# Second graph-attention layer: the logits of a block's first three columns made by TensorE, a block ahead

## Chip, cores and metric

One Trainium2 chip, one of its cores. The metric is the device time of one execution in microseconds, the median of several runs. Engines are named as in the profile: PE (TensorE, with PEld its weight loads), DVE (VectorE), ACT (ScalarE), POOL (GpSimd), SP (the queue that issues plain DMAs).

## The reference

A graph of 6250 nodes with 256 features each and 100000 directed edges, sorted by destination. Two layers of attention of one kind (GATv2, four heads of 64), a residual and a layer norm, then one layer of another kind (eight heads of 32), a residual and a layer norm:

```
def _gatv2_layer(x, src, dst, n, Wl, Wr, att, b):
    xl = (x @ Wl).reshape(n, 4, 64);  xr = (x @ Wr).reshape(n, 4, 64)
    e = leaky_relu(xl[src] + xr[dst], 0.2)
    logits = einsum('ehc,hc->eh', e, att)
    ex = exp(logits - segment_max(logits, dst)[dst])
    alpha = ex / segment_sum(ex, dst)[dst]
    return segment_sum(xl[src] * alpha[:, :, None], dst).reshape(n, 256) + b

h = elu(_gatv2_layer(x, ..., Wl1, Wr1, att1, b1))      # layer 1, with an edge from each node to itself
h = _gatv2_layer(h, ..., Wl2, Wr2, att2, b2)           # layer 2, the same edges
x = layernorm(x + h)
x = layernorm(x + third_layer(x, W, a, src, dst))      # a GAT layer with logits s1[src] + s2[dst]
```

The change concerns the line `logits = ...` of layer 2.

## The kernel before

All arithmetic is in float32. A plan made at the start sorts the nodes by the number of their edges, most first, and cuts them into 49 blocks of 128. A block's nodes lie on the 128 partitions, and a block has as many columns as its nodes may have edges, and one more ahead of them (column 0) for the node's own row: 28 in block 0, then 26, 25, 24, 23, 22, 22, 21 (three blocks), 20 (four), 19 (four), 18 (four), 17 (five), 16 (five), 15 (five), 14 (four), 13 (three), 12 (two), 11 (two) and 10 in block 48. The few edges of block 0 that do not fit are dealt with apart (the `few_...` names).

A column's rows are fetched by one indirect DMA of POOL (`gather_rows`, L1300): 128 rows of 260 numbers, four heads of 64 and a 65th each, which carries the linear part of the leaky ReLU. Column 0 isn't gathered; ACT copies it from a tile `two` (L1712), which SP loads. The columns of a block are cut into two to four tiles `g` of at most nine columns, as equal as can be, from one pool of nine such tiles. So the gathers run ahead of the arithmetic until all nine are full.

`layer2` is called twice, with i=0 for layer 1 and i=1 for layer 2. The order of instructions on every engine is the order in which the program is written; each engine works off its own queue and waits only for the data that it needs. One turn of the loop over blocks b does, in this order:

1. the gathers of block b+1 are issued, and `own2` copies its destination rows `xr` into PSUM (`ready`, L1711);
2. `attend(b)`: for each tile, DVE takes the maximum of the rows and `xr` (L1573), multiplies by the attention vector `at` (L1574) and sums each head (L1575) into the logits `lg`; then DVE takes the largest (`top`, L1439), and ACT the exponentials, one call a head (L1446), into `wt`. After them ACT copies some of the weights (`by`, L1453) and, from the list `later`, the own row of block b+1 into column 0 of that block's first tile (L1712);
3. `end(b - 1)`: DVE divides the last block's sum `acc` by `den` (L1602), adds the residual (L1715) and takes its mean and variance (L1516, L1518), and ACT the reciprocal of the deviation (L1520, L1521);
4. DVE's reciprocal of `den` (L1638), and `weighted_sum`: DVE multiplies the first tile by its weights (L1477); then comes the call `between()`, in which DVE makes the shift of the layer norm (`sd`, L1525) and ACT applies it (L1528); then the other tiles, of the last one a part by ACT (L1476). PE sums the columns into `acc` with an identity (L1484);
5. PE turns the normalised block (L1420) and multiplies it for the third layer (L1427), ACT copies the result out (L1726) and SP stores it (L1728).

PSUM tiles for turning and for products come from one pool `pst`, with the tag `tp`, of two buffers that are used in turn.

The third layer gathers rows that the second one stored. For its first three blocks 37 gathers (`begin`, from the call `follow`) need no rows of the last four blocks; the others wait for all of them.

Of the kernel before, what the change touches and what calls it, by code (L numbers as in the profile page):

```python
# [26 lines left out]
F32 = mybir.dt.float32  # L27
# [3 lines left out]
OP = mybir.AluOpType  # L31
AX = mybir.AxisListType
# [3 lines left out]
P = 128  # L36
# [4 lines left out]
RUNS = 64  # L41
EARLY = (14, 12, 11)
LATE = 4


def columns(E, N, NB):
# [1161 lines left out]
def tile_by_degree(  # L1208
# [3 lines left out]
    nc = tc.nc  # L1212
    N, F = x.shape
    H2, D2 = att1.shape
    H1, _, D1 = w3.shape
    NB = -(-N // P)
    NP = NB * P
    T = 9
    A1 = F + H1
    W2 = H2 * (D2 + 1)  # L1220
    CM = near_d.shape[1] - F
# [8 lines left out]
    def per_head(t, H):  # L1230
        return t.rearrange("p (h d) -> p h d", h=H)
# [9 lines left out]

    AHEAD = (NB - LATE) * P
    KEY = max(cols).bit_length()
# [4 lines left out]
                   allow_small_or_imprecise_dtypes=True)  # L1248
# [3 lines left out]
                   allow_small_or_imprecise_dtypes=True)  # L1252
# [42 lines left out]
    def gather_rows(b, rows, cut, own, table, of, width, j0, j1):  # L1295


        for g, (s0, s1) in zip(rows, cut):
            for j in range(max(s0 - own, j0), min(s1 - own, j1)):
                nc.gpsimd.indirect_dma_start(  # L1300
                    out=g[:, j + own - s0, :width], out_offset=None, in_=table,
                    in_offset=source(of, b, j),
                )
# [31 lines left out]
    def gather_few(table, j, width):  # L1335
        nc.gpsimd.indirect_dma_start(
            out=few_row[:, :width], out_offset=None, in_=table,
            in_offset=bass.IndirectOffsetOnAxis(ap=few_at[:, j : j + 1], axis=0),
        )
# [38 lines left out]
    def row_tiles(b, own):  # L1378
        cut = chunks(cols[b] + own)
        return [rowp.tile([P, T, RW], F32, name="g") for _ in cut], cut  # L1380
# [149 lines left out]
    def layer2(i, table, of, width, start, own, finish, follow):  # L1530

        with ExitStack() as es:
            zp = es.enter_context(tc.tile_pool(name=f"z{i}", bufs=1))
            work = es.enter_context(tc.tile_pool(name=f"work{i}", bufs=3))
            ps = es.enter_context(tc.tile_pool(name=f"ps{i}", bufs=2, space=PSUM))
            ps1 = es.enter_context(tc.tile_pool(name=f"ps1{i}", bufs=1, space=PSUM))  # L1540
            pst = es.enter_context(tc.tile_pool(name=f"pst{i}", bufs=2, space=PSUM))
            at = ps1.tile([P, W2], F32, name="at")
            nc.scalar.copy(at, att[i])
            state = {}

            def gather(b):
                first = EARLY[b] if b in begun else 0
                rows, cut = begun.pop(b) if first else row_tiles(b, 1)
                gather_rows(b, rows, cut, 1, table, of, width, first, cols[b])
                if b == 0:  # L1550
                    gather_few(table, i, width)
                state[b] = [rows, cut]

            later = []

            def ready(b):
                pr, put = own(work, ps, pst, b, state[b][0][0][:, 0, :W2])
                state[b].append(pr)
                later.append(put)

            def attend(b):
                rows, cut, xr = state.pop(b)
                S = cols[b] + 1
                lg = work.tile([P, CM + 1, H2], F32, name="lg")
                if b == 0:
                    own_r = work.tile([P, W2], F32, name="few_own", bufs=1)
                    nc.scalar.copy(own_r, xr)
                    po = pst.tile([P, W2], F32, name="few_r", tag="tp")
                    nc.tensor.matmul(po, node_of, own_r, start=True, stop=True)
                for g, (s0, s1) in zip(rows, cut):  # L1570
                    n = s1 - s0
                    z = zp.tile([P, T, W2], F32, name="z")[:, :n, :]
                    nc.vector.tensor_max(z, g[:, :n, :W2], xr[:, None, :].to_broadcast([P, n, W2]))  # L1573
                    nc.vector.tensor_mul(z, z, at[:, None, :].to_broadcast([P, n, W2]))  # L1574
                    nc.vector.reduce_sum(  # L1575
                        lg[:, s0:s1, :], z.rearrange("p t (h d) -> p t h d", h=H2), axis=AX.X
                    )
                if b == 0:
                    none(po)
                    z = zp.tile([P, T, W2], F32, name="z")[:, 0, :]  # L1580
                    nc.vector.tensor_max(z, few_row[:, :W2], po)
                    nc.vector.tensor_mul(z, z, at)
                    few_lg = work.tile([P, H2], F32, name="few_lg", bufs=1)
                    nc.vector.reduce_sum(few_lg, per_head(z, H2), axis=AX.X)
                    few_logits(work, pst, lg, few_lg, H2)
                    if i == 0:
                        nc.vector.tensor_copy(few_at[:, 1:], few_row[:, W2 : W2 + 1])
                few = min(S // 3, cut[-1][1] - cut[-1][0] - 1) if b + 1 < NB else 0
                wt, new = weights(work, ps, lg, S if b else S + FEW, H2, few, S)
                while later:  # L1590
                    later.pop()()
                if i == 0:
                    for g, (s0, s1) in zip(rows, cut):
                        s = max(s0, 1)
                        nc.scalar.copy(spots[:, b, s - 1 : s1 - 1], g[:, s - s0 : s1 - s0, W2])
                    if 0 < b <= len(EARLY):
                        sort_sources(work, pst, b - 1)
                return rows, cut, wt, new

            def end(b, acc, den):  # L1600
                h = work.tile([P, F], F32, name="h")
                nc.vector.tensor_mul(  # L1602
                    per_head(h, H2), per_head(acc, H2),
                    den.unsqueeze(2).to_broadcast([P, H2, D2]),
                )
                if i == 0:
                    nc.vector.tensor_add(h, h, bias[0])
                return finish(work, pst, b, h)

            for b in range(3):  # L1610
                if (i, b) not in loaded:
                    start(b)
            if i == 0:
                find_few(work, pst)
            gather(0)
            ready(0)
            later.pop()()
            if i == 0:
                none(state[0][2])
            acc, den, rest = None, None, None  # L1620
            for b in range(NB):
                if b + 3 < NB:
                    start(b + 3)
                if b + 1 < NB:
                    gather(b + 1)
                if b + 2 == NB:
                    follow()
                if b + 1 < NB:
                    ready(b + 1)
                rows, cut, wt, new = attend(b)  # L1630
                if b:
                    rest = end(b - 1, acc, den)
                else:
                    few = few_sum(work, pst, wt[0], cols[0] + 1, H2, D2 + 1)
                if i == 0:
                    nc.vector.tensor_add(x1[:, b, :], x1[:, b, :], bias[1])
                den = new()
                nc.vector.reciprocal(den, den)  # L1638

                last = []  # L1640

                def between():
                    if b:
                        last.append(rest())

                acc = weighted_sum(
                    ps1, rows, cut, wt, H2, D2 + 1, between, b == 0,
                )
                if b == 0:
                    nc.tensor.matmul(acc, edges_of, few, start=False, stop=True)  # L1650
                if i == 0 and b + 1 < NB:
                    none(state[b + 1][2])
                if last:
                    last[0]()
            end(NB - 1, acc, den)()()

    def none(t):

        nc.vector.memset(t.rearrange("p (h d) -> p h d", h=H2)[:, :, D2:], -BIG)
# [76 lines left out]
    def begin2():  # L1736
        begin(1, xl2_d, W2)
        for b in range(3):
            start2(b)
            loaded.add((1, b))  # L1740

    layer2(0, xl1_d[:, :], sources, W2 + 1, start1, own1, finish1, begin2)
    last_weights()
    layer2(1, xl2_d[:, :], spots, W2, start2, own2, finish2, lambda: begin(0, wh_d, A1))

    with ExitStack() as es:
        work = es.enter_context(tc.tile_pool(name="work3", bufs=3))
        ps = es.enter_context(tc.tile_pool(name="ps3", bufs=3, space=PSUM))
        state = {}
# [59 lines left out]
        for b in range(NB):  # L1809
# [4 lines left out]
            rows, cut, wt, new = attend(b)  # L1814
# [46 lines left out]
```

## Time and profile before

| | |
|---|---|
| median of 3 runs | 3349.63 us (3349.41 to 3349.76) |
| the profiled execution | 3349.41 us, span 3347.6 us |
| busy, share of the span | DVE 85%, POOL 73%, PE 40%, PEld 32%, ACT 31% |
| layer 2 on DVE | from 1241.85 us (first maximum, block 0) to 2294.82 us (last statistics) |
| first third-layer gather that needs the last rows | 2302.9 us |
| gathers, L1300 | 0.95 us each |
| L1573, L1574, L1575, both layers | 497 us busy each, 234 instructions each |

A profile shows one execution. A group's row gives line, engine, operation, what is written and read, and the count, then busy time and the mean of one, then the idle time of the engine ahead of it and what ended that. A row of the timeline gives start, duration, engine, line and shape. In a row of waits stand the engine and line that waited, what it waited for, the total in us, how often, and the longest. "issue" is time in which an engine waited for nothing that the profile shows. PEclk is the share of full clock that PE was granted.

### The profile page before, as it was taken

What the parts mean: (1) busy time and instruction counts of PE and PEld (TensorE: products, weight loads), DVE (VectorE), ACT (ScalarE), POOL (GpSimd) and SP (SyncE); (2) the same over time, 40 slices, a digit from 0 to 9 for tenths busy, and PEclk for the clock granted to TensorE, in tenths of its full rate; (3) what the DMA queues carried; (4) which work ended last, traced back from release to release, by engine and by line L of the source; (5) the groups of instructions that cost most, each with busy time, mean ns of one, the idle gap of its engine ahead of it and who ended that gap; (6) DMA issues with size and microseconds to landing.
All of it is one profiled execution on the core that took longest, in us unless ns stands there. A gap on an engine that the chain in (4) does not pass through costs nothing.

```text
span 3347.6 us, 23565 instructions
## 1 busy us (share of the span) xinstructions
PE 1350.1 (40%) x5129; PEld 1076.3 (32%) x5130; DVE 2858.4 (85%) x2674; ACT 1048.7 (31%) x4176; POOL 2439.5 (73%) x2588
## 2 busy tenths in 40 slices
PE   7355665666667753554545555553000000000000
PEld 6244554555555543443434444442000000000000
DVE  7699999999999979999999999995976666666766
ACT  3133444444454532443444444451000000000000
POOL 5477777777777777777777777647777777777775
PEclk8678888888888876777777777776555555555555
DMA  8744444444444454444444444434433343333333
GB/s 203 145 111 117 117 121 118 119 120 121 122 122 122 123 137 111 121 121 123 114 126 127 126 126 127 112 94 114 108 107 108 107 108 108 107 108 107 108 107 86
DMA packets 189101, 395.81 MB, mean 118 GB/s; under 512 B 56249, under 2 KB 107963, under 8 KB 188934
## 3 DMA queue, kind: packets, MB, share of 16 engines
q0 software_dynamic: 121392, 339.19, 38.8%
q1 hardware_dynamic: 59858, 53.27, 5.5%
q10 hardware_dynamic: 7700, 1.74, 0.4%
q8 instruction: 45, 0.74, 0.1%
q14 instruction: 106, 0.87, 0.1%
HBM read 354.02 MB, written 40.42 MB: 118 GB/s over the span
## 4 chain that ended last, share of the span: by engine, by line
POOL 21%; DVE 20%; issue 14%; DMA 3%; PE 2%; ACT 2%; DVEq 0%; POOLq 0%; ACTq 0%
POOL g L1300 20%; DVE z L1574 5%; DVE z L1573 5%; DVE lg L1575 5%; PE acc L1484 2%; DVE g L1477 2%; DMA g<-xl_d,near_r 2%; ACT wt L1446 2%; POOL out L1800 1%; DMA out<-y,node_i 1%; DVE weighted L1497 1%; DMA g<-whs_d,near_r 0%; DVE top L1439 0%; DVE acc_v L1506 0%; DVE sd L1525 0%
## 5 line engine op out<-in xcount | busy, mean ns | idle before, releaser
L1300 POOL DMA_INDIRECT g<-xl_d,near_r x1569 | 1487.7, 948 | 518.6 <-issue 425.8
L1484 PE MATMUL acc<-g,ident 128*128 128x256 f32 x3408 | 968.0, 454 | 750.1 <-DVE sd L1525 443.1
L1484 PEld LDWEIGHTS acc<-g,ident 128*128 128x128 f32 x3408 | 787.7, 234 | 931.1 <-issue 478.3
L1300 POOL DMA_INDIRECT g<-whs_d,near_r x766 | 726.8, 949 | 233.9 <-issue 226.9
L1573 DVE TENSOR_TENSOR z<-g,pr 128x1820 f32<-128x1820 f32 (+4 forms) x234 | 497.2, 2125 | 20.8 <-DMA g<-xl_d,near_r 7.4
L1574 DVE TENSOR_TENSOR z<-z,at 128x1820 f32<-128x1820 f32 (+4 forms) x234 | 497.5, 2126 | 8.0
L1575 DVE TENSOR_REDUCE lg<-z 128x28 f32<-128x1820 f32 (+4 forms) x234 | 497.3, 2125 | 8.1
L1476 ACT ACTIVATE g<-g,by 128x64 f32<-128x64 f32 x2056 | 500.0, 334 | 0.0
L1477 DVE TENSOR_TENSOR g<-g,wt 128x1792 f32<-128x1792 f32 (+8 forms) x234 | 348.3, 1505 | 2.7
L1506 DVE TENSOR_REDUCE acc_v<-weighted 128x256 f32<-128x4096 f32 (+15 forms) x49 | 343.7, 7014 | 1.6
L1446 ACT ACTIVATE wt<-lg,top 128x19 f32<-128x19 f32 (+14 forms) x392 | 115.3, 294 | 496.3 <-DVE top L1439 460.2
L1456 ACT ACTIVATE wt<-lg 128x128 f32<-128x128 f32 (+17 forms) x49 | 14.0, 285 | 802.0 <-DVE lg L1455 802.0
L1770 DVE TENSOR_TENSOR lg<-g,s_r 128x56 f32<-128x56 f32 (+4 forms) x111 | 22.4, 214 | 268.1 <-DMA g<-whs_d,near_r 212.3
L1497 DVE TENSOR_TENSOR weighted<-g,wt 128x1792 f32<-128x1792 f32 (+4 forms) x111 | 226.6, 2057 | 0.1
L1422 ACT COPY xT<-pt 128x256 f32<-128x256 f32 x147 | 55.0, 374 | 498.0 <-PE pt L1420 498.0
L1427 PE MATMUL pm<-wcat,xT 128*128 128x260 f32 x392 | 100.8, 401 | 22.6 <-ACT xT L1422 22.6
L1427 PEld LDWEIGHTS pm<-wcat,xT 128*128 128x128 f32 x392 | 71.5, 192 | 43.4 <-ACT xT L1422 34.4
L1446 ACT ACTIVATION_READ_ACCUMULATOR wt<-lg,top 128x1 f32 x392 | 73.1, 186 | 0.0
L1800 POOL DMA_INDIRECT out<-y,node_i x49 | 50.0, 1021 | 25.9 <-issue 14.2
L1427 PE MATMUL pm<-wh_cat,xT 128*128 128x272 f32 x196 | 58.8, 423 | 22.6 <-ACT xT L1422 22.6
L1427 PE MATMUL pl<-wcat,xT 128*128 128x260 f32 x196 | 57.4, 416 | 25.2 <-ACT xT L1422 25.2
L1691 ACT COPY row<-pm 128x260 f32<-128x260 f32 x98 | 36.6, 374 | 86.9 <-PE pm L1427 86.9
(247 smaller groups left out, 1436.8 us busy)
## 6 DMA issues: line engine op xcount, KB each, us to landing
g<-xl_d,near_r POOLq DMA_INDIRECT x1569, 2.8
g<-whs_d,near_r POOLq DMA_INDIRECT x766, 2.8
whs_d<-row SPq DMA_DIRECT2D x49, 132.0 KB, 2.0
xl_d<-xl SPq DMA_DIRECT2D x49, 130.0 KB, 6.0
xl_d<-row SPq DMA_DIRECT2D x49, 130.0 KB, 2.5
xr_d<-row SPq DMA_DIRECT2D x49, 130.0 KB, 3.1
two<-xl_d SPq DMA_DIRECT2D x49, 130.0 KB, 3.1
two<-xr_d SPq DMA_DIRECT2D x49, 130.0 KB, 3.2
```

What stands on the lines that cost most here:

```text
L1300: nc.gpsimd.indirect_dma_start(out=g[:, j + own - s0, :width], out_offset=None, in_=table, in_offset=source(of, b, j),)
L1427: nc.tensor.matmul(pm, xT[:, c, :], w[:, c, :], start=c == 0, stop=c == 1)
L1446: nc.scalar.activation(wt[:, :, h], lg[:, :S, h], AF.Exp, bias=top[:, h : h + 1], accum_out=den[:, h : h + 1],)
L1476: nc.scalar.mul(g4[:, t, h, :], g4[:, t, h, :], by[:, t - m, h : h + 1])
L1477: nc.vector.tensor_mul(g4[:, :m], g4[:, :m], wt[:, s0 : s0 + m, :].unsqueeze(3).to_broadcast([P, m, H, F // H]),)
L1484: nc.tensor.matmul(acc, ident, g4[:, t], start=s0 + t == 0, stop=s0 + t == S - 1 and not more)
L1497: nc.vector.tensor_mul(prod[:, s0 - base : s1 - base, :].rearrange("p t (h d) -> p t h d", h=H), g[:, :n, :F].rearrange("p t (h d) -> p t ...
L1506: nc.vector.reduce_sum(part, prod[:, : s1 - base, :].rearrange("p s f -> p f s"), axis=AX.X)
L1573: nc.vector.tensor_max(z, g[:, :n, :W2], xr[:, None, :].to_broadcast([P, n, W2]))
L1574: nc.vector.tensor_mul(z, z, at[:, None, :].to_broadcast([P, n, W2]))
L1575: nc.vector.reduce_sum(lg[:, s0:s1, :], z.rearrange("p t (h d) -> p t h d", h=H2), axis=AX.X)
L1800: put = nc.gpsimd.indirect_dma_start(out=out[:, :], out_offset=node(b), in_=y, in_offset=None, bounds_check=N - 1, oob_is_err=False,)
```

## The change

For i=1 alone, the logits of columns 0, 1 and 2 of a block are no longer made by DVE in `attend`, but by PE. A new function `turn(b + 1)` is called in the turn of block b, between `end(b - 1)` and the reciprocal. DVE takes the maximum of the three columns; PE transposes each column in three parts (128, 128 and 4 of the 260 numbers) into a PSUM tile `pz` (tag `tp`), ACT copies it to SBUF in two copies, and PE multiplies the turned parts by `at_of`, which holds the attention vector spread over four columns, one a head. The twelve logits of a node are copied from PSUM into `lg` by DVE, at the head of `between()`. In `attend` the three passes skip the three columns. For block 0 `turn` and the copy stand ahead of the loop. `at_of` is made once, before the loop, by three small products, an iota on POOL and seven small operations of DVE.

```diff
+TURNED = 3
...
             at = ps1.tile([P, W2], F32, name="at")
             nc.scalar.copy(at, att[i])
+            turns = TURNED if i == 1 else 0
+            parts = [(c, min(W2, c + P)) for c in range(0, W2, P)]
+            if turns:
+                at_c = work.tile([P, len(parts)], F32, name="at_c", bufs=1)
+                nc.vector.memset(at_c, 0.0)
+                for c, (f0, f1) in enumerate(parts):
+                    pa = pst.tile([P, 1], F32, name="pa", tag="tp")
+                    nc.tensor.matmul(
+                        pa[: f1 - f0], att[i][:, f0:f1], ident[:, :1], start=True, stop=True
+                    )
+                    nc.vector.tensor_copy(at_c[: f1 - f0, c : c + 1], pa[: f1 - f0])
...
+                nc.gpsimd.iota(
+                    place, pattern=[[P, len(parts)], [-(D2 + 1), H2]], base=0,
+                    channel_multiplier=1, allow_small_or_imprecise_dtypes=True,
+                )
...
+                nc.vector.tensor_mul(at_of, at_of, at_c.unsqueeze(2).to_broadcast(shape))
...
+            logits = {}
+            def turn(b):
+                rows, cut, xr = state[b]
+                zt = work.tile([P, turns, W2], F32, name="z_turn", bufs=2)
+                nc.vector.tensor_max(
+                    zt, rows[0][:, :turns, :W2], xr[:, None, :].to_broadcast([P, turns, W2])
+                )
+                turned = []
+                for t in range(turns):
+                    pz = pst.tile([P, len(parts), P], F32, name="z_t", tag="tp")
+                    zT = work.tile([P, len(parts), P], F32, name="zT", bufs=turns)
+                    for c, (f0, f1) in enumerate(parts):
+                        nc.tensor.transpose(pz[: f1 - f0, c, :], zt[:, t, f0:f1], ident)
+                    full = W2 // P
+                    nc.scalar.copy(zT[:, :full], pz[:, :full])
+                    if W2 % P:
+                        nc.scalar.copy(zT[: W2 % P, full], pz[: W2 % P, full])
+                    turned.append(zT)
+                by_at = pst.tile([P, turns, H2], F32, name="by_at", tag="tp")
+                for t, zT in enumerate(turned):
+                    for c, (f0, f1) in enumerate(parts):
+                        nc.tensor.matmul(
+                            by_at[:, t, :], zT[: f1 - f0, c, :], at_of[: f1 - f0, c, :],
+                            start=c == 0, stop=c == len(parts) - 1,
+                        )
+                logits[b] = work.tile([P, CM + 1, H2], F32, name="lg")
+                return lambda: nc.vector.tensor_copy(logits[b][:, :turns, :], by_at)
...
                 for g, (s0, s1) in zip(rows, cut):
                     n = s1 - s0
-                    z = zp.tile([P, T, W2], F32, name="z")[:, :n, :]
-                    nc.vector.tensor_max(z, g[:, :n, :W2], xr[:, None, :].to_broadcast([P, n, W2]))
-                    nc.vector.tensor_mul(z, z, at[:, None, :].to_broadcast([P, n, W2]))
+                    m = turns if s0 == 0 else 0
+                    z = zp.tile([P, T, W2], F32, name="z")[:, : n - m, :]
+                    nc.vector.tensor_max(
+                        z, g[:, m:n, :W2], xr[:, None, :].to_broadcast([P, n - m, W2])
+                    )
+                    nc.vector.tensor_mul(z, z, at[:, None, :].to_broadcast([P, n - m, W2]))
                     nc.vector.reduce_sum(
-                        lg[:, s0:s1, :], z.rearrange("p t (h d) -> p t h d", h=H2), axis=AX.X
+                        lg[:, s0 + m : s1, :], z.rearrange("p t (h d) -> p t h d", h=H2), axis=AX.X
                     )
...
+            if turns:
+                turn(0)()
             acc, den, rest = None, None, None
             for b in range(NB):
...
+                begun_turn = turn(b + 1) if turns and b + 1 < NB else None
                 den = new()
                 nc.vector.reciprocal(den, den)
                 last = []
                 def between():
+                    if begun_turn:
+                        begun_turn()
                     if b:
                         last.append(rest())
```

More of the change, by code (lines that the diff above doesn't have):

```diff
@@ L1543, in layer2 @@
             nc.scalar.copy(at, att[i])
+            turns = TURNED if i == 1 else 0
[9 more added lines that the diff above has]
+                    nc.vector.tensor_copy(at_c[: f1 - f0, c : c + 1], pa[: f1 - f0])
+                shape = [P, len(parts), H2]
+                place = work.tile(shape, F32, name="at_place", bufs=1)
+                nc.gpsimd.iota(
+                    place, pattern=[[P, len(parts)], [-(D2 + 1), H2]], base=0,
+                    channel_multiplier=1, allow_small_or_imprecise_dtypes=True,
+                )
+                at_of = work.tile(shape, F32, name="at_of", bufs=1)
+                nc.vector.tensor_single_scalar(at_of, place, 0.0, op=OP.is_ge)
+                nc.vector.scalar_tensor_tensor(
+                    at_of, place, float(D2 + 1), at_of, op0=OP.is_lt, op1=OP.mult
+                )
+                nc.vector.tensor_mul(at_of, at_of, at_c.unsqueeze(2).to_broadcast(shape))
             state = {}
@@ L1563, in attend @@
                 S = cols[b] + 1
-                lg = work.tile([P, CM + 1, H2], F32, name="lg")
+                lg = logits.pop(b) if turns else work.tile([P, CM + 1, H2], F32, name="lg")
                 if b == 0:
@@ L1571, in attend @@
                     n = s1 - s0
-                    z = zp.tile([P, T, W2], F32, name="z")[:, :n, :]
-                    nc.vector.tensor_max(z, g[:, :n, :W2], xr[:, None, :].to_broadcast([P, n, W2]))
-                    nc.vector.tensor_mul(z, z, at[:, None, :].to_broadcast([P, n, W2]))
+                    m = turns if s0 == 0 else 0
+                    z = zp.tile([P, T, W2], F32, name="z")[:, : n - m, :]
+                    nc.vector.tensor_max(
+                        z, g[:, m:n, :W2], xr[:, None, :].to_broadcast([P, n - m, W2])
+                    )
+                    nc.vector.tensor_mul(z, z, at[:, None, :].to_broadcast([P, n - m, W2]))
                     nc.vector.reduce_sum(
-                        lg[:, s0:s1, :], z.rearrange("p t (h d) -> p t h d", h=H2), axis=AX.X
+                        lg[:, s0 + m : s1, :], z.rearrange("p t (h d) -> p t h d", h=H2), axis=AX.X
                     )
```

## The prediction

> **What bounds the kernel now.** I read the page first, then, for the second layer's stretch alone (1241 to 2296 us), the waits of VectorE and of GpSimd, then one block of it in order of time, then the clock around that block. From the page:
>
> ```profile
> PE 1350.1 (40%) x5129; PEld 1076.3 (32%) x5130; DVE 2858.4 (85%) x2674; ACT 1048.7 (31%) x4176; POOL 2439.5 (73%) x2588
> ```
>
> DVE is busiest, POOL next. Which of them paces the second layer is told by who waits there. DVE's waits, 1262 to 2310 us (engine and line, what it waited for: us in total, times, longest):
>
> ```profile
> DVE den L1638 <- ACT wt L1446: 17.1, 48, 0.4
> DVE h L1602 <- PE acc L1484: 5.7, 1, 5.7
> DVE few_weight L1368 <- PE few_w L1363: 3.3, 1, 3.3
> ```
>
> POOL's, 1262 to 2255 us:
>
> ```profile
> POOL g L1300 <- issue: 205.6, 675, 0.3
> POOL g L1300 <- PE acc L1484: 45.9, 36, 6.1
> ```
>
> DVE waits 0.36 us a block for the exponentials and otherwise only at the first and last block, never for a gathered row. POOL issues a gather each 1.25 us (0.95 busy, 0.30 "issue") and gives up some 35 us more waiting for PE to free a row tile: it runs ahead until the nine tiles are full. So DVE paces this layer, closely followed by POOL, and a microsecond added to DVE's queue in each block is a microsecond on the end; one removed is a gain as long as POOL's slack lasts. The third layer's gathers begin with the last rows of this one (2302.9 us), so the difference is carried to the end whole.
>
> DVE and ACT in a block of 17 columns (start, us, engine, line, operation):
>
> ```profile
> 1897.46 0.27 DVE L1439 TENSOR_REDUCE top<-lg 128x4 f32<-128x68 f32 x1
> 1899.01 0.18 DVE L1518 BATCH_NORM_AGGREGATE mv<-stats 128x2 f32<-128x6 f32 x1
> 1899.55 0.18 DVE L1638 RECIPROCAL den<-den 128x4 f32<-128x4 f32 x1 [0.36 <-ACT wt L1446]
> 1899.69 0.41 ACT L1712 COPY g<-two 128x260 f32<-128x260 f32 x1
> 1899.76 2.29 DVE L1477 TENSOR_TENSOR g<-g,wt 128x2048 f32<-128x2048 f32 x1
> 1901.97 0.15 DVE L1525 SCALAR_TENSOR_TENSOR sd<-mv,sd 128x1 f32<-128x1 f32 x1
> ```
>
> To be seen: the new maximum of `turn` comes between the second and third of these lines, the new copy of the logits between the last two. The fourth line is ACT's copy of the next block's own row into column 0 of that block's first tile; the maximum reads that column. PE is idle here, and its clock down (stretch, length, busy us and count of PE, PEld, DVE, ACT, POOL, then the granted clock):
>
> ```profile
> 1896.00:1900.00 4.00, 0.00 (x0) 0.00 (x0) 3.48 (x8) 2.11 (x10) 3.00 (x4) 0.50 0.54 154
> 1902.00:1904.00 2.00, 1.80 (x4) 1.52 (x5) 2.00 (x4) 1.85 (x7) 1.39 (x3) 0.50 0.37 108
> 1906.00:1908.00 2.00, 2.00 (x11) 1.77 (x10) 1.97 (x2) 1.53 (x7) 1.39 (x3) 1.00 0.32 90
> ```
>
> **What it removes.** In each of 49 blocks the three passes over the first tile (L1573 to L1575) lose three columns. The rows of 1300 and 2340 elements take 1.502 and 2.590 us: 0.272 us a column and 0.14 fixed. The instructions stay; 3 x 3 x 0.272 = 2.45 us a block go.
>
> **What it puts on DVE.** (a) The maximum over three columns: 0.14 + 3 x 0.272 = 0.96 us. It can't start when DVE is free (1899.2) but when the own row is copied, 1899.69 + 0.41 = 1900.10, plus 0.05 for the signal (as from ACT's 1234.31 to PE's 1234.36). It ends at 1901.11, and the reciprocal, which now starts at 1899.55, at 1901.13: 1.58 us later. In blocks at 1363 and 2226 us the same working gives 1.52 and 1.51; I take 1.55. DVE's 0.36 us wait is in this already. (b) The copy of 12 logits from PSUM: no such row; nearest are one-element and 11-element ones at 0.15 to 0.17. I take 0.17. (c) The wait at that copy, which stands behind the multiply of the block's first tile and ahead of everything else on DVE. From the end of the maximum DVE has work of its own for 0.21 (reciprocal to multiply) and one multiply. By first tile, the multiplies are 2.553, 2.286, 2.019, 1.752 and 1.49 us for 9, 8, 7, 6 and 5 columns, in 4, 13, 16, 13 and 2 of the 48 blocks: mean 2.04, so a cover of 2.25 us. If the chain from the maximum's end to the logits takes C, DVE stands C - 2.25.
>
> Sum for a block: -2.45 + 1.55 + 0.17 + C - 2.25 = C - 2.98. All hangs on C; the logits are made a block ahead, but DVE asks for them in the block in which they are begun.
>
> **The chain C.** PE, at clock 0.50 after 7 us of idleness, turns column 0 in three pieces of 128, 128 and 4. Two such transposes at that clock (1233 us, ahead of L1422) took 0.79 us from DVE's end to ACT's start; two overlapped ones took 0.69 together and 0.478 each, so a third adds 0.21: ACT starts at 1.0. ACT's two copies: a 264-element one lets the next start 0.28 later, and a 128-element one ends some 0.28 after that: 1.56. ACT has nothing else then (its next work in the block waits for DVE's `sd`). Column 1 is turned meanwhile; column 2 needs the first of the two PSUM buffers back, so it starts at 1.6 and PE is through with it at 2.3; its copies are done at 3.2, before its products come. Then 9 products in fp32, which the trace shows as two loads and two matmuls each (3408 for acc, 852 columns in each of two layers): 18 pairs. No row has pairs with four moving columns in such a number. Nearest is this one, with 12 columns, at clock 0.50:
>
> ```profile
> 129.55 0.60 PE L1323 MATMUL few_k<-few_got,node_of 128*128 128x12 f32 x2 [1.03 <-DVE node_of L1319]
> ```
>
> Two in 0.60 at 0.38 each: 0.22 apart. At clock 1.00 two transposes take 0.38 at 0.273 each: 0.11 apart. All at the low clock: 2.3 + 18 x 0.22 + 0.22 for the last one's end and the signal = 6.5. With the clock up 3.7 us after PE began, as for acc here (1902.2 to about 1905.9): 6.4 pairs until then, 11.6 x 0.11 after, C = 5.2. Bounds: all at 1.00, 0.79 to the first copy, PE through with column 2 near 2.0 and 18 x 0.11 after, 4.2; every pair as long as one low-clock load (0.338, acc at 1902.8), 2.3 + 6.1 + 0.2 = 8.6. I take 5.9, between the two middle ones, since the pairs with four columns leave PE's array mostly empty and may not raise the clock as acc does.
>
> [...]
>
> **Beside the path.** ACT gets six copies, about 1.3 us a block, in a pause of 1.6 us before L1528; what DVE's wait delays is `sd`, then L1528, the scaled columns and acc's second tile, about 4.5 us later in the block. acc of this block would end near 1912.3, and DVE asks for it near 1920: covered by over 7 us (in the last blocks by 4). PE's acc queue behind the turn has the same cover. POOL gets tiles back later and waits more, which costs nothing while DVE paces; its new iota stands before the second layer's own gathers, in 1.2 us of waiting for the last row's write. The maximum asks for columns 1 and 2 a block early: POOL, stopped by full tiles, is two blocks ahead. The setup (three small products, seven small DVE operations) lies in DVE's 5.2 us wait at 1241.85. Nothing covers the first turn: 0.96 + 5.9 + 0.17 - 2.45 = 4.6 us; I count 4, as part of that wait may be used.
>
> **Sum.** 48 x (5.9 - 2.98) = 140, and 4: 144 us. The profiled execution took 3349.41 us (span 3347.6, 1.8 around it), 0.2 under the median, so 3493.
>
> **The rivals.** (1) The chain is short because PE is at full clock: C = 4.2, 59 + 4 = 63 us, 3412. Against it: PE has been idle 7 us and is at 0.50 in 1896 to 1900. With part of the way to 5.2, chance 0.17. (2) The low clock and load-bound pairs: C from 7.2 to 8.6, 207 to 274 us, 3556 to 3624. For it: low-clock loads of 0.338; against it: few_k's two are 0.22 apart. Chance 0.15. (3) Faster: the logits are there when DVE comes for them. From C = 2.98 down the sum turns; with C at 2.25 no wait is left and the block gains 0.73, 48 x 0.73 = 35 us less 1 at the start, 3316. For it: DVE is the pace, and its busy time does fall, by 1.3 us a block. Against it: column 2's copies end at 3.2, and its six pairs can't begin before. Chance 0.04. (4) C within 0.14 of 2.98, no difference: 0.02. My forecast, C from 4.8 to 7.2, has 0.62.
>
> A difference under 0.2% (6.7 us) can't be told from none. The range reaches from part of rival 1 (C = 4.5, 3427) into rival 2 (C = 7.6, 3575).
>
> **What would show it.** DVE's wait at the new copy: 3.6 us a block on PE, about 175 us over the layer; its wait ahead of the new maximum: 0.9 us a block on ACT's L1712; DVE's busy time down by about 60 us; third-layer gathers beginning 144 us later at the same pace; POOL's waits for acc up by over 100 us. It is wrong if the copy waits under 1 us, if the block pitch at 17 columns (20.6 us now) falls or rises by far from 2.9, or if the maximum waits for gathers instead.

## The result, and the profile after

The changed kernel takes 3541.12 us (median of five runs, 3539.07 to 3543.21) against 3349.76 us: a ratio of 1.057 (95% interval 1.0559 to 1.0582), 191 us slower. Forecast were 3493 us and 3427 to 3575. Its profiled execution took 3543.21 us with a span of 3541.4 us, 193.8 us more than the one before. The experiments e5 to e12 ran on two other chips (e12 on the second), on which the kernel before took 3814 to 3827 us; each is compared alone with the kernel before that was run beside it. e2 to e5, e7, e8 and e10 are one run each.

The busy times on the page of the changed kernel, the line that answers to the one shown of before:

```profile
PE 1672.2 (47%) x6459; PEld 1354.9 (38%) x6459; DVE 2785.6 (79%) x2779; ACT 1124.2 (32%) x4470; POOL 2441.1 (69%) x2589
```

DVE has 73 us less to do and is idle 267 us more. What it waits for, from 1250 to 2490 us (engine and line, what it waited for: us in total, times, longest):

```profile
DVE lg L1616 <- PE by_at L1611: 234.2, 49, 6.7
DVE z_turn L1594 <- ACT g L1777: 45.5, 45, 2.6
DVE h L1662 <- PE acc L1485: 6.2, 1, 6.2
```

The wait for the exponentials, 17.1 us before, is nearly gone (2.2); in its place stand two new ones. 234.2 us fall to the copy of the twelve logits, 4.78 us a block; 45.5 us to the maximum's wait for the own row. One block in order of time shows both, a block of 16 columns whose turn serves another of 16 (start, us, engine, line, operation; in brackets the idle time ahead and what ended it):

```profile
2025.89 0.41 ACT L1777 COPY g<-two 128x260 f32<-128x260 f32 x1
2026.33 0.97 DVE L1594 TENSOR_TENSOR z_turn<-g,pr 128x780 f32<-128x780 f32 x1 [0.93 <-ACT g L1777]
2027.21 0.17 DVE L1701 RECIPROCAL den<-den 128x4 f32<-128x4 f32 x1
2027.30 2.26 DVE L1478 TENSOR_TENSOR g<-g,wt 128x2048 f32<-128x2048 f32 x1
2027.44 2.39 PE L1602 MATMUL z_t<-ident,z_turn 128*128 128x128 f32 x9 [5.19 <-DVE z_turn L1594]
2028.35 0.37 ACT L1604 COPY zT<-z_t 128x256 f32<-128x256 f32 x1 [1.62 <-PE z_t L1602]
...
2029.62 4.40 PE L1611 MATMUL by_at<-at_of,zT 128*128 128x4 f32 x18
...
2033.94 9.63 PE L1485 MATMUL acc<-g,ident 128*128 128x256 f32 x32
2034.05 0.17 DVE L1616 COPY lg<-by_at 128x12 f32<-128x12 f32 x1 [4.50 <-PE by_at L1611]
```

To be seen: the maximum ends at 2027.30 and the logits come at 2034.05, a chain of 6.75 us. DVE has 2.25 us of other work and stands for 4.50. The chain is the same in every block: from 6.70 to 6.76 us in all 49. Before, the shift L1525 of this block came 19.81 us after that of the block ahead of it (1901.97); the same step, now L1526, takes 23.35 us, 3.54 more:

```profile
1921.78 0.15 DVE L1525 SCALAR_TENSOR_TENSOR sd<-mv,sd 128x1 f32<-128x1 f32 x1
```

```profile
2010.79 0.15 DVE L1526 SCALAR_TENSOR_TENSOR sd<-mv,sd 128x1 f32<-128x1 f32 x1
2034.14 0.15 DVE L1526 SCALAR_TENSOR_TENSOR sd<-mv,sd 128x1 f32<-128x1 f32 x1
```

The clock over the chain and after it (stretch, length, busy us and count of PE, PEld, DVE, ACT, POOL, then the granted clock):

```profile
2027.40:2029.60 2.20, 2.16 (x9) 1.40 (x10) 2.15 (x1) 1.04 (x4) 1.59 (x3) 0.50 0.37 104
2032.50:2034.00 1.50, 1.50 (x8) 1.46 (x7) 0.00 (x0) 0.00 (x0) 1.15 (x2) 0.50 0.44 133
2036.00:2038.00 2.00, 2.00 (x7) 1.55 (x6) 1.97 (x2) 2.00 (x10) 0.00 (x0) 0.50 0.18 52
2038.00:2040.00 2.00, 2.00 (x9) 1.69 (x8) 1.93 (x3) 1.70 (x8) 0.00 (x0) 0.76 0.02 4
2040.00:2044.00 4.00, 3.79 (x19) 3.09 (x17) 3.97 (x2) 0.17 (x1) 2.84 (x3) 1.00 0.25 67
```

PE is busy by the profile from 2027.4 on, but its clock stays at 0.50 through the whole chain. It goes up near 2039, when acc, with 256 columns a matmul, has run for some 5 us. Over the layer it goes up 2.9 to 6.2 us after acc begins (48 blocks, mean 4.7). In the kernel before, where PE is idle ahead of acc, it does so after 2.9 to 6.0 us (48 blocks, mean 4.4). So here 6.6 us of transposes and four-column products ahead of acc brought the clock up no sooner (mean 4.7) than an idle PE did (4.4).

GpSimd and the start of the third layer:

```profile
POOL g L1301 <- PE acc L1485: 214.6, 43, 13.4
```

```profile
2496.73 0.94 POOL L1301 DMA_INDIRECT g<-whs_d,near_r  x1 [11.39 <-DMA whs_d<-row]
```

GpSimd waits for free tiles 169 us longer than before. The first gather that needs the last rows comes at 2496.73 and not at 2302.9: 193.8 us later, just the difference of the spans. 3.7 us of it were there at the end of layer 1, whose work is the same (its last L1662 at 1232.28 against L1602 at 1228.56); 190 us arose in layer 2.

The account of these 190 us: stand at the copy 234; wait for the own row and, twice, for gathers 47; the maximum and the copy on DVE, 49 x (0.88 + 0.09) by the distances of starts, 48; the wait for the exponentials -15; the columns removed, 49 x 2.45, -120. The sum is 194, 4 more than arose.

### The profile page after: what moved, and what is told of

Same layout as the page of the kernel before. It is cut to its first block, busy times and chain, and to the rows that moved or that the text cites. A ratio compares the mean times of both kernels' runs of the same rounds, so it can differ in the third digit from the quotient of the medians.

```text
span 3541.4 us, 26771 instructions
## 1 busy us (share of the span) xinstructions
PE 1672.2 (47%) x6459; PEld 1354.9 (38%) x6459; DVE 2785.6 (79%) x2779; ACT 1124.2 (32%) x4470; POOL 2441.1 (69%) x2589
## 5 line engine op out<-in xcount | busy, mean ns | idle before, releaser
L1631 DVE TENSOR_TENSOR z<-g,pr 128x1820 f32<-128x1820 f32 (+7 forms) x234 | 457.3, 1954 | 17.1 <-DMA g<-xl_d,near_r 7.9
L1634 DVE TENSOR_TENSOR z<-z,at 128x1820 f32<-128x1820 f32 (+7 forms) x234 | 457.6, 1956 | 8.1
L1635 DVE TENSOR_REDUCE lg<-z 128x28 f32<-128x1820 f32 (+7 forms) x234 | 457.5, 1955 | 8.0
L1602 PE MATMUL z_t<-ident,z_turn 128*128 128x128 f32 (+1 forms) x441 | 116.9, 430 | 309.6 <-DVE z_turn L1594 307.6
L1498 DVE TENSOR_TENSOR weighted<-g,wt 128x1792 f32<-128x1792 f32 (+4 forms) x111 | 226.6, 2056 | 0.1
L1611 PEld LDWEIGHTS by_at<-at_of,zT 128*128 128x128 f32 (+1 forms) x882 | 209.4, 317 | 16.0 <-ACT zT L1606 11.6
L1611 PE MATMUL by_at<-at_of,zT 128*128 128x4 f32 (+1 forms) x882 | 215.3, 357 | 0.0
L1602 PEld LDWEIGHTS z_t<-ident,z_turn 128*128 128x128 f32 (+1 forms) x441 | 66.5, 184 | 355.8 <-issue 326.8
L1616 DVE COPY lg<-by_at 128x12 f32<-128x12 f32 x49 | 8.4, 171 | 234.2 <-PE by_at L1611 234.2
L1604 ACT COPY zT<-z_t 128x256 f32<-128x256 f32 x147 | 54.8, 372 | 108.2 <-PE z_t L1602 102.4
```

The costliest lines, as they stand in the source:

```text
L1498: nc.vector.tensor_mul(prod[:, s0 - base : s1 - base, :].rearrange("p t (h d) -> p t h d", h=H), g[:, :n, :F].rearrange("p t (h d) -> p t ...
L1602: nc.tensor.transpose(pz[: f1 - f0, c, :], zt[:, t, f0:f1], ident)
L1611: nc.tensor.matmul(by_at[:, t, :], zT[: f1 - f0, c, :], at_of[: f1 - f0, c, :], start=c == 0, stop=c == len(parts) - 1,)
L1631: nc.vector.tensor_max(z, g[:, m:n, :W2], xr[:, None, :].to_broadcast([P, n - m, W2]))
L1635: nc.vector.reduce_sum(lg[:, s0 + m : s1, :], z.rearrange("p t (h d) -> p t h d", h=H2), axis=AX.X)
```

## The experiments

The theory: DVE paces the second layer; it stands at the copy because it asks there, in the block in which the chain is begun, for what PE and ACT need 7 us to make. Against it stood that PE's own load delays acc, that the wait for the own row is hidden, and that GpSimd is the pace.

**e2, the own row made early.** ACT copies it at the start of the block's turn:

```diff
                 state[b].append(pr)
-                later.append(put)
+                if turns:
+                    put()
+                    later.append(lambda: None)
+                else:
+                    later.append(put)
```

> As changed, but ACT copies the next block's own row at the start of the block's turn, not after the exponentials, so the maximum of the turn need not wait for it. Theory (the 0.9 us that DVE waits for the own row ahead of the maximum is on the path, as it comes before the chain): 48 x 0.9 = 43 us less than changed, about 3497; the stand at the copy stays near 4.8 us. Rival (the wait is hidden, since the chain is bound by something that starts later): unchanged, 3535 to 3545, the stand at the copy grows by 0.9.

Measured: 3496.11 us, 45 less than changed (143 over the kernel before beside it, 3353.12, where changed is 191 over its own: 48 by that). DVE's waits, 1262 to 2440 us:

```profile
DVE lg L1620 <- PE by_at L1615: 224.0, 48, 5.0
...
DVE z_turn L1598 <- ACT g L1781: 1.6, 2, 1.0
```

The own-row wait is gone, the stand at the copy is unchanged (4.7 us a block). So the own-row waits were on the path, as the chain begins after them.

**e4, 12 pairs and not 18.** The products with the four-row parts are left out:

```diff
-                    for c, (f0, f1) in enumerate(parts):
+                    for c, (f0, f1) in enumerate(parts[:2]):
...
-                            start=c == 0, stop=c == len(parts) - 1,
+                            start=c == 0, stop=c == 1,
```

> As changed, but the products with the third part of each column, which contract four rows, are left out: 12 pairs instead of 18 (the last four of the 260 numbers are missing from the three columns' logits). Theory (a pair costs the same whether it contracts 4 or 128 rows, 0.243 us): the chain is 6 x 0.243 = 1.46 us shorter, 48 x 1.46 = 70 us, about 3471. Rival (four-row loads are nearly free): 3530 to 3541.

Measured: 3454.76 us, 86 less than changed. The products and the copy of a block like the one shown:

```profile
2002.75 2.67 PE L1611 MATMUL by_at<-at_of,zT 128*128 128x4 f32 x12
...
2005.46 0.17 DVE L1616 COPY lg<-by_at 128x12 f32<-128x12 f32 x1 [2.77 <-PE by_at L1611]
```

The stand fell from 4.50 to 2.77 here and from 234 to 149.5 us in all: 85 us, the whole gain. What the chain loses on PE, DVE gains. Twelve pairs take 2.67 to the end of the last one, 0.222 each, and their starts lie 0.21 apart, near the 0.22 that the prediction took from `few_k`. The other six had taken 4.40 - 2.67 = 1.73, 0.288 each: in this chain they are dearer than full ones, not only as dear. By the single starts in the changed kernel's trace the two four-row pairs of a column lie 0.24 apart, and the steps from a full pair to a four-row one and back are 0.28 each; the loads themselves are no longer (0.28 to 0.33 us as drawn, against 0.33). With all 18 pairs at the mean of 0.243 us, 70 us would have gone.

**e3, PE kept at work ahead of the turn.**

```diff
                 rows, cut, wt, new = attend(b)
+                if turns and b + 1 < NB:
+                    fill = pst.tile([P, 2, P], F32, name="fill", tag="tp")
+                    for k in range(13):
+                        nc.tensor.matmul(fill, ident, x1[:, 0, :], start=True, stop=True)
```

> As changed, with 13 extra fp32 products of 256 columns a block on PE between the third-layer product and the turn, into a PSUM tile that nobody reads, so that PE is not idle for the 5 us before the turn. Theory (the granted clock of 0.50 through the whole chain makes the 18 pairs 0.243 us apart instead of 0.11): the clock is 1.00 in the chain, its 18 pairs take near 2.2 instead of 4.4 us, the stand falls to about 2.3 us, time about 3425. Rival (a pair with four columns costs its load, 0.24 us apart at either clock): only the transposes gain, the stand stays over 4 us, 3510 to 3540.

Measured: 3489.51 us, 52 less than changed, between the two expectations (56 us of the stand are gone: 178.0 in all). A block in which the extra products (to 2012.8) reached up to the turn:

```profile
2014.46 2.62 PE L1611 MATMUL by_at<-at_of,zT 128*128 128x4 f32 x18
...
2017.11 0.17 DVE L1616 COPY lg<-by_at 128x12 f32<-128x12 f32 x1 [2.09 <-PE by_at L1611]
```

and its clock:

```profile
2014.00:2016.00 2.00, 1.96 (x15) 1.75 (x15) 1.02 (x1) 0.92 (x4) 1.46 (x2) 1.00 0.36 87
2016.00:2018.00 2.00, 2.00 (x11) 1.83 (x12) 0.89 (x3) 0.62 (x2) 1.39 (x3) 0.83 0.39 112
2018.00:2020.00 2.00, 2.00 (x6) 1.55 (x6) 1.97 (x3) 2.00 (x9) 1.70 (x2) 0.50 0.43 106
```

At clock 1.00 the 18 pairs take 2.62 us, 0.146 each, and the stand is 2.09. And the clock didn't last: 0.83 from 2016 to 2018, between 1.00 and 0.50, means that it fell at about 2017.3, just after the last pair, though PE was busy by the profile for 3.91 of the 4.20 us from 2012.9 to 2017.1. In the block of the maximum at 1833 us, where the extra products end 1 us before the turn, it falls among the pairs (0.61 from 1836 to 1838), and the chain takes 5.65 us. From 1800 to 2200 us the stand is 47.1 us over 19 blocks, 2.5 each, against 76.2 over 17 in the changed kernel, 4.5 each. From 1300 to 1800, where blocks are longer and the 13 products end 2.7 us and more before the turn, it is 79.7 over 17, 4.7 each, against 4.8. So the clock is worth 2.0 us a block where it can be had; a stand of 2.1 us is left with the clock up throughout.

**e1, the copy late.** PE writes the logits into the next block's own weight tile, and DVE copies them after that block's passes:

```diff
-                by_at = pst.tile([P, turns, H2], F32, name="by_at", tag="tp")
+                S = cols[b] + 1 if b else cols[0] + 1 + FEW
+                wts[b] = ps.tile([P, S + turns, H2], F32, name="wt")
+                by_at = wts[b][:, S:, :]
...
+                if b in made:          # in attend, after the loop over tiles
+                    made.pop(b)()
...
-                    if begun_turn:     # in between()
-                        begun_turn()
```

> The twelve logits are written by PE into the next block's own weight tile in PSUM, and DVE copies them after that block's passes over its tiles instead of at the head of the call between(); all else as changed. Theory (DVE stands 4.8 us a block at the copy because it asks in the block in which the chain is begun, and nothing else costs): the stand of 234 us vanishes, each block stands at -2.45 + 1.55 + 0.17 = -0.73 us against before, 48 blocks -35 us, so 3310 to 3325 us, below the kernel before. Rival A (PE's chain of 7 us a block itself delays acc until acc is the bound): the wait moves to L1662 on acc, and the time stays over 3400. Rival B (GpSimd's gathers, 1.25 us each, take over as the pace at once): about 3345 to 3350, with DVE waiting for gathers.

Measured: 3427.33 us, a ratio of 1.0221 (1.0204 to 1.0238) to the kernel before at 3353.12. 114 us less than changed, but not under the kernel before: the theory had said 3310 to 3325. DVE's waits, 1240 to 2480 us:

```profile
DVE z_turn L1594 <- ACT g L1781: 117.6, 46, 3.3
DVE h L1667 <- PE acc L1485: 49.4, 27, 6.2
```

The stand at the copy has gone altogether; in its place DVE waits 2.6 us a block for the own row, and in 27 blocks for acc. Why the own row is late, in order of time:

```profile
1943.78 3.40 PE L1485 MATMUL acc<-g,ident 128*128 128x256 f32 x15
...
1947.21 0.42 DVE L1667 TENSOR_TENSOR h<-acc,den 128x256 f32<-128x256 f32 x1 [1.34 <-PE acc L1485]
1947.43 0.37 ACT L1423 COPY xT<-pt 128x256 f32<-128x256 f32 x1 [8.33 <-PE pt L1421]
...
1951.60 0.41 ACT L1781 COPY g<-two 128x260 f32<-128x260 f32 x1
...
1952.04 0.97 DVE L1594 TENSOR_TENSOR z_turn<-g,pr 128x780 f32<-128x780 f32 x1 [3.26 <-ACT g L1781]
```

In this block it is a ring: acc stands behind the chain on PE and ends late (1947.2); ACT, which waits 8.33 us for it, can copy the turned block only then, and only after it come the exponentials, the own row and with it the next turn, whose chain again stands ahead of acc. Rival A, that PE's chain delays acc, is right in kind, though its price (over 3400) is shared between two waits. Rival B fell: the maximum of the turn waits 0.9 us in all for gathered rows. In the changed kernel DVE waits for acc only once (6.2 us); there it stands at the copy while acc is worked off.

**e5 to e12, on the slower chips.** e5 joins e1 and e2. e6 issues the turn after the passes over the first tile of the block before, so that PE does it behind the third-layer product, and queues what a block begins with ahead of that product; e9, e11 and e12 queue it ahead of the multiply by the weights. In short, for e9:

```diff
                     nc.vector.reduce_sum(
                         lg[:, s0 + m : s1, :], z.rearrange("p t (h d) -> p t h d", h=H2), axis=AX.X
                     )
+                    if s0 == 0 and turns and b + 1 < NB:
+                        made[b + 1] = turn(b + 1)
...
+                if turns and b + 1 < NB:
+                    prepare(b + 1)     # gathers, loads, own2 of the turn after
                 acc = weighted_sum(
```

e7 and e10 drop the turn:

```diff
-                zt = work.tile([P, turns, W2], F32, name="z_turn", bufs=2)
...
-                return lambda: nc.vector.tensor_copy(logits[b][:, :turns, :], by_at)
+                return lambda: nc.vector.memset(logits[b][:, :turns, :], 0.0)
```

and e8 turns one column (`TURNED = 1`). In e7 and e10 the logits of three columns are left out, so their results are not the layer's. What was expected of e5 to e12, in this order:

> The edits of e1_copy_late and e2_own_row_early together. e1 came out at 3427 and not near 3316: DVE there waits 2.5 us a block for the own row, because ACT gets to it late, behind the third-layer copies that wait for acc, and PE does acc only after the 18 pairs. Theory (a ring: acc late, ACT late, own row late, turn late, acc late): without the own row in the ring DVE waits for acc itself, 18 us round (1.9 to the maximum, 1.0, 6.6 chain, 8.6 acc), no longer than DVE's own work of a block of 16 columns, so 3300 to 3345. Rival (only the own-row wait goes, the rest of the ring stays): 3427 - 46 x 0.95, near 3383, with DVE waiting for acc over 2 us a block.

> As e5, but the turn of block b+1 is issued after the passes over the first tile of block b, ahead of its exponentials, and what a block's turn begins with (gathers, loads, the copies of destination rows and own row) is queued ahead of the third-layer product of the block before. PE then does the turn after acc and the third-layer product, in its pause and while its clock is still at 1.00, with a whole block to spare. Theory (DVE paces, its work falls by 2.45 - 0.9 - 0.1 = 1.45 us a block, nothing waits any more; GpSimd's 35 us of waiting and the tail are the limit): 3285 to 3315, DVE's waits under 30 us in the layer, some of them for gathered rows. Rival A (PE's chain still delays acc, as in e1): over 3350. Rival B (GpSimd is the pace already): 3335 to 3350.

> As changed, without the turn: DVE's passes skip three columns, and the logits of these are set to zero; no maximum, transposes, copies or products (the logits of three columns are left out). Theory (DVE paces, with GpSimd close behind): 2.45 us a block leave DVE, 120 us in all, but GpSimd needs 1.25 us for each of 766 gathers after 1241 us and 46 us for 37 more before the third layer can go on, so the gain stops at 45 to 75 us: 3275 to 3305, with DVE now waiting for gathers. Rival (GpSimd has enough slack): 3230 to 3240, DVE waits for nothing.

> As changed, with one column turned instead of three. Theory (DVE's wait is the chain less its cover of 2.25 us): the chain is 1.0 for the transposes, 0.6 for ACT, 4 pairs at 0.22 and 2 at 0.29, 0.3 for ends: 3.3, so a wait of 1.1 us; per block -0.82 (removed) + 1.0 (reciprocal later, own row and maximum) + 0.17 + 1.1 = 1.45, 48 x 1.45 = 70 and 3 at the start: about 3425. Rival (the cost goes with the number of columns, one third of the change's): 3349 + 64 = 3413 or less, down to 3380, with the own-row wait hidden.

> As e6, with the next blocks' gathers, loads and own-row copies queued ahead of the multiply by the weights, so that ACT makes the own row before its scaled columns and not after them (in e6 DVE stood 3.4 us a block for it). Theory: DVE waits for nothing in the layer but gathered rows; its work falls by 1.45 us a block, so up to 70 us, and GpSimd's pace (1.25 us a gather) stops the gain at 45 to 60: 3285 to 3310 on a chip where the kernel before takes 3350, a ratio of 0.980 to 0.988. Rival A (PE's 5 us of turn a block still push acc): DVE waits for acc, ratio over 1.00. Rival B (GpSimd is the pace already): 0.995 to 1.00, DVE's waits for gathers take up all that was saved.

> The kernel of e7_no_turn again, for a chip at the usual speed: as changed, without the turn; the logits of three columns are left out (zero). Theory (DVE paces, GpSimd close behind): 45 to 75 us less than before, 3275 to 3305, with DVE waiting for gathered rows. Rival (GpSimd has enough slack): 120 us less, 3230 to 3240.

> The kernel of e9 again, for a chip at the usual speed (the kernel before near 3350; in e5 to e10 it took 3820, with ACT and PE standing for their own instructions). Theory: nothing that DVE asks for comes late; its work falls by 1.45 us a block, and GpSimd's pace stops the gain at 45 to 60 us: 3285 to 3310, ratio 0.980 to 0.988. Rival A (PE's 5 us of turn a block still push acc): DVE waits for acc, ratio over 1.00. Rival B (GpSimd is the pace already): 0.995 to 1.00, DVE's waits for gathers take up what was saved.

> The kernel of e9 and e11 once more, in the hope of a chip at the usual speed (before near 3350). There, by the theory that DVE paces the layer with GpSimd close behind, 3285 to 3310; by the rival that PE's turn still pushes acc, over 3350; by the rival that GpSimd is the pace already, 3335 to 3350. On a chip where the kernel before takes 3800 and more, a ratio of 1.00 to 1.01, as in e9 and e11, and nothing is learnt of the three.

| | us | kernel before beside it |
|---|---|---|
| e5 | 3879.44 | 3826.36 |
| e6 | 3887.02 | 3826.36, ratio 1.016 (1.013 to 1.0189) |
| e7 | 3847.41 | 3826.36 |
| e8 | 3843.01 | 3826.36 |
| e9 | 3833.58 | 3821.01, ratio 1.0035 (1.0016 to 1.0054) |
| e10 | 3829.07 | 3821.01 |
| e11 | 3849.39 | 3814.32, ratio 1.0086 (1.0065 to 1.0108) |
| e12 | 3868.27 | 3825.53, ratio 1.0105 (1.008 to 1.0129) |

The times answer nothing that was asked: in e7 and e10 DVE is busy for 2744 us and not for 2858 as before, and nothing is gained. When they ran, DVE was not the pace. What is slow there begins ahead of the change: the first maximum of the turn comes at 1445 to 1466 us and not at 1244 as in the changed kernel, after a first layer whose program is the same, and the third layer's gathers take 1.04 us each (e9, e12) and not 0.95. In e9's page ACT stands ahead of its scaled columns (both layers):

```profile
L1477 ACT ACTIVATE g<-g,by 128x64 f32<-128x64 f32 x2056 | 565.3, 338 | 454.8 <-issue 451.4
```

455 us idle ahead of 2056 instructions, for nothing that the profile shows; before and after, on the first chip, it was 0.0. What makes ACT stand there is open, and so is whether it lies with the chips. Whether e7's 45 to 75 us and e9's 3285 to 3310 would come out at the usual speed is open too.

The waits inside these runs can still be read. e8: DVE's stand for one column's logits (1400 to 2750 us):

```profile
DVE lg L1616 <- PE by_at L1611: 40.9, 36, 3.0
```

1.14 us each, where the sum by the pairs gave 1.1 for one column. e5, the same stretch:

```profile
DVE h L1671 <- PE acc L1485: 111.3, 47, 8.3
```

With the own row early, DVE's largest wait is for acc, 2.4 us each: the other half of the ring, as the rival had it (over 2 us a block), though on a chip that is slow in other ways too. In e6 DVE waited 148.0 us for the own row, which ACT made after its scaled columns; in e9, where ACT makes it before them, the wait for the own row has no line left among DVE's waits, and at the copy (L1623) 27.1 us are left, 15.6 put down to acc and 11.5 to "remote", for which the trace names no instruction. So in e9 DVE hardly stands for the chain any more; that this would hold where nothing else holds DVE up is not shown. What e9 waits for most is the exponentials:

```profile
DVE den L1715 <- ACT wt L1447: 161.1, 36, 20.4
```

## Why the prediction was right, and what was mis-sized

- **DVE paces the layer, and a microsecond of its queue is one at the end.** Held: what arose in layer 2 was carried whole to the third layer's first gather, and e2 and e4 each gave back what they took from DVE's waits (45 for 47, 86 for 85). On the slower chips it did not hold (e7, e10).
- **What is removed and added on DVE.** The maximum took 0.97 (0.96 said), the copy 0.17 (0.17), the wait for the own row 0.93 in the block shown (0.95), the reciprocal's wait vanished in it.
- **The sum for a block** has the right terms. In the block shown, as measured: -2.45, the reciprocal 1.45 later (0.93 + 0.88 - 0.36), 0.09 for the copy, a stand of 4.50: 3.59; the pitch rose by 3.54.
- **C was mis-sized**, the step that took 5.9 between 5.2 (the clock rises after 3.7 us, or 3.5 by the 0.58 of 1904 to 1906 in that view) and 6.5 (it does not). The chain is 6.75 us, and in all 49 blocks the clock stays near 0.50 through it (0.51 at most). Of the two weighed there, the higher is what the runs show, pairs that did not raise the clock, and the middle should have been left to it: 0.6 us. That PE's array stands mostly empty, the ground given for it, was the author's estimate; no run shows how full it is. The other 0.3 us lie with the pairs, whose starts are 0.238 apart on average and not 0.22, because the four-row ones are dearer. 48 x 0.86 is 41 of the 47 us missed.
- **The cover of the copy was mis-sized** as well, by less: 2.02 us on average and not 2.25. The multiply starts where the maximum is drawn to end (2027.30 for both) and not 0.21 us behind it. That is 11 us more; the copy, which moves DVE's next start by 0.09 and not 0.17, takes 4 back. So the stand, forecast at 3.65 us a block, is 4.74 without the first one.
- **The cover of acc and ACT.** DVE waits for acc once, at the end (6.2 us, before 5.7), but the cover was less than the 7 us forecast: in the block shown acc ends at 2043.57 and DVE asks for it at 2046.94. The prediction let acc end near 1912.3, 0.8 us later than before, although it begins only when the chain is through. For ACT the cover ran out in the last stretch (2300 to 2500 us): DVE's wait for the own row is 11.6 us in 7 blocks there, 1.7 each and not 0.93. In one of them ACT copies the turned block, which stands behind acc, only at 2434.60, and so begins the exponentials at 2436.89, 1.8 us after DVE's `top`, and the own row behind them.
- **The first turn** cost 6.7 us of standing; the layer's first pass came 6.5 us later by layer 1's end, 4 after the columns saved, as said.
- **The clock.** The value 5.2 let it rise 3.7 us after PE began, and PE began with the transposes. Here PE was busy by the profile for 6.6 us (2027.4 to 2034.0) at 0.50, and the clock rose 5 us after matmuls of 256 columns began (2033.94, near 2039). Over the layer that took 4.7 us on average, against 4.4 in the kernel before, where PE is idle ahead of them. So in these traces the time that the profile draws as busy did not tell when the clock rises.
- **Rival 1 (short chain)** fell: C was 6.75 and not 4.2; e3 shows what it takes (chain 4.3 from the maximum's end at 2012.77 to the copy at 2017.11). **Rival 2 (load-bound pairs)** had its place right, the low clock, but not its price: 0.21 to 0.28 from pair to pair and not 0.338. **Rival 3 (faster)** is excluded where the copy stands, and e1 shows that hiding the copy alone isn't enough.

## What to carry to other kernels

Work that is moved to another engine "a block ahead" is hidden only if the result is asked for a block later: look for the place of the instruction that reads it in its engine's queue, and set the chain against the work between. Count a chain of small matmuls by instructions (two a product in fp32, 0.21 to 0.28 us a pair here) and at the low clock (0.50 here), since here they didn't raise it. When the reader is moved out of the way, ask next what stood behind the chain on its own engine, and what waits for that in order on the others.

## What was not expected of the hardware

- Transposes and matmuls with four moving columns, 6.6 us of them in which PE is drawn as busy, left the clock at 0.50, and it rose no sooner after the start of the wide products behind them (mean 4.7 us) than behind an idle PE (4.4). In e3 it fell from 1.00 at about 2017.3, 4.5 us after the last wide product (2012.8), with PE busy in nearly all the time between. How much of this lies with the transposes and how much with the narrow products no run separates.
- In this chain of products that contract 128 rows, those that contract four cost more: 0.288 us a pair against starts 0.21 apart at clock 0.50, with 0.28 at each step from the one kind to the other.
- The same kernel before took 3350 us in the main runs, 3353 beside e1 to e4, and 3814 to 3827 on two other chips; there e9 has 455 us of ACT's idle time ahead of instructions that waited for nothing shown. In these runs a gain on DVE didn't show: e7 and e10, with 114 us less for DVE, came out 21 and 8 us over the kernel before.
